# Cross-attention block on one core: the third batch's MLP by Strassen's scheme behind attention, with its rows kept in DRAM

## The chip, the cores and the metric

The kernel runs on one core of a Trainium2 chip. The core has TensorE (matrix products, in the profile PE, its weight loads PEld), VectorE (DVE), ScalarE (ACT), GpSimd (POOL) and SyncE (SP, here only a queue that issues transfers). Each engine works through its own instructions in order and waits for others by semaphores. The metric is the time of one execution in device microseconds; the median of several runs is compared.

## The reference

All values are fp32; batch 4, 512 rows, width 512, 16 heads of 32, inner width 2048.

```python
x = layer_norm(hidden_states, ln1_w, ln1_b)
q = (x @ q_w + q_b) ; k = (enc @ k_w + k_b) ; v = (enc @ v_w + v_b)   # split into 16 heads
attn = softmax(where(mask, q k^T / sqrt(32), min))
hidden = (attn v) @ cproj_w + cproj_b + hidden_states
y = layer_norm(hidden, ln2_w, ln2_b)
y = gelu(y @ fc_w + fc_b, approximate=True)
return hidden + y @ proj_w + proj_b
```

## The kernel before, in words

**Attention.** The work is cut into 16 groups w: batch b = w // 4 and four heads. A group has four units, one for each 128 query rows; unit u = 4 w + qt, 64 in all. A unit is `scores` (L207): four 32-row products into the single PSUM tile `sc`, VectorE's mask and row minimum of each head (L219, which frees `sc`), ScalarE's exp (L223), and then `turn` (L227), which transposes the four tiles. VectorE does this in 32x32 blocks (L251), and sixteen transfers on SP's queue (L274) put the blocks of two units (a pair) into the one tile `pT`; three pairs are transposed on TensorE instead and four use other tiles. `attend` (L297) multiplies a pair by v, four units after its first unit, and then VectorE multiplies by the inverse row sums (L322), the last reader of `pT`. Only then may the next pair's transfers start.

**The filler.** Between a unit's parts TensorE gets other work, in chains of four products of 512 columns: `prep_k`, `prep_q`, `prep_v` (three chains a group, three groups ahead), `cproj` of the batch that has just been attended (four chains and a VectorE sum into the row tiles `hid`), the second norm with its transposes (`ln2`, `ln2_turn`), and the MLP of the batch before: 16 `fc` chains (L377 on; gelu on ScalarE) and 16 `proj` chains (L390 on; a VectorE sum into `hid`, the last of which is stored). The lists `first[w]` are run from a group's first unit on, `later[w]` is added at the group's third unit. `run` takes items while their nominal costs (3.4 a chain, 0.5 a turn) fit into a quarter of the group's total, half of it before `turn` and half behind. The order that results is the order of every engine's queue: nothing is moved afterwards.

**Loads.** Weights are loaded by Pool's queue (`load_w`, `load_fc`, `load_p`, `load_hid`), each into a slot that its former reader must have left; Pool waits for that in its own order. `wk`, `wq` and `wv` have two slots each and are loaded together, one group ahead. `hid` has six slots, filled with the rows of x, to which Pool adds a bias (L339); a second bias is added on Pool after the norm (`proj_bias`, L362). The slots that are filled anew wait for the output store.

**The last MLP.** Batch 3's MLP has no attention beside it and is done by Strassen's scheme (Winograd's form): seven products of half-size blocks instead of eight. `fc_pair` (L466) does two of fc's 16 blocks; for it Pool forms four sums of the weight blocks (`a_sums`), VectorE four sums of y (`b_sums`, L555) and the sums of the products. `project` (L505) does the whole proj as seven products of 16 matmuls for each of two row tiles; the sums of the weights (`p_sums`) are Pool's, those of gelu's output (`g_sums`) VectorE's. The weights are loaded by SP's queue, pair by pair.

The norm of rows (`ln_stat`, `ln_rs`, `ln_norm`, L102 to L120) is: two VectorE instructions for each of four row tiles, two on Pool for rs, and four norms on VectorE.

Of the kernel before, what the change touches and what calls it, by code (L numbers as in the profile page):

```python
# [50 lines left out]
AHEAD = 3  # L52
LAG = 4
# [13 lines left out]
def xattn_block(ctx: ExitStack, tc: tile.TileContext, x, encT, mask, q_w, k_w, v_w, c_w, fc_w, p_w, vecs, rows, out):  # L67
# [6 lines left out]
    const, keep, hids, tiles, small = pools(ctx, const=1, keep=1, hids=6, tiles=4, small=4)  # L74
    ps_acc = ctx.enter_context(tc.tile_pool(name="ps_acc", bufs=4, space=PSUM))
# [90 lines left out]
    def load_w(w, queue=nc.gpsimd, names=("wk", "wq", "wv")):  # L166

        g = w % NG
        for n, src in (("wk", k_w), ("wq", q_w), ("wv", v_w)):
            if n in names:  # L170
                S[n, w] = two.tile([P, ND, P], F32, tag=n, name=f"{n}_{w}")
                queue.dma_start(out=S[n, w], in_=src[:, g, :, :])
# [10 lines left out]
    def prep_q(w):  # L183
        b, g = divmod(w, NG)
        qT = kqp.tile([P, L], F32, tag="qT", name=f"qT_{w}")
        acc = acc_tile(f"accq_{w}")
        for d in range(ND):
            nc.tensor.matmul(acc, S["wq", w][:, d, :], xT[:, d, :], start=(d == 0), stop=(d == ND - 1))  # L188

        nc.scalar.activation(qT, acc, AF.Identity, bias=qb[:, g : g + 1], scale=-scale)  # L190
        S["qT", w] = qT

    def prep_v(w):
# [3 lines left out]
        for t in range(NT):  # L197
            for d in range(ND):
                nc.tensor.matmul(  # L199
                    acc[:, ts(t, P)], eT[:, d, ts(t, P)], S["wv", w][:, d, :],  # L200
                    start=(d == 0), stop=(d == ND - 1),
                )
        nc.scalar.copy(v, acc.rearrange("p (t f) -> p t f", t=NT))
# [129 lines left out]
    def load_hid(b, ts_):  # L333

        for t in ts_:
            S["hid", b, t] = hids.tile([P, D], F32, tag="hid", name=f"hid_{b}_{t}")
            nc.gpsimd.dma_start(out=S["hid", b, t], in_=x[b, ts(t, P), :])
# [3 lines left out]
    def cproj(b, t):  # L341
# [3 lines left out]
        h = S["hid", b, t]  # L345
        nc.vector.tensor_tensor(h, acc, h, ALU.add)
        ln_stat((2, b), t, h)

    def ln2(b):
        if b + 1 < B:  # L350
# [4 lines left out]
        for t in range(NT):  # L355
            h = S["hid", b, t]
            ln_norm((2, b), t, S["yn", b][t], h)
# [6 lines left out]
    def ln2_turn(b, d):  # L364
        if d == 0 and b + 1 < B:
# [7 lines left out]
    def load_p(b, f):  # L373
        S["pw", b, f] = tiles.tile([P, D], F32, tag="pw", name=f"pw_{b}_{f}")
# [31 lines left out]
    def last_mlp(b, before):  # L406
# [5 lines left out]
        NP = NF // 2  # L412
        HL = L // 2

        last, ring = pools(ctx, last=1, ring=2)
        ps_last = ctx.enter_context(tc.tile_pool(name="ps_last", bufs=4, space=PSUM))

        yT = S["yT", b] = keep.tile([P, ND, L], F32, tag="yT", name=f"yT_{b}")
        ys = last.tile([P, 4, 2, HL], F32, tag="ys", name="ys")

# [3 lines left out]
        pt4 = last.tile([P, NP, HL], F32, tag="pt4", name="pt4")  # L424
        pt12 = gt[:, : 2 * NP * HL].rearrange("p (i c n) -> p i c n", i=2, c=NP)

# [3 lines left out]
        def sub(engine, o, x0, x1):  # L430
            engine.tensor_tensor(o, x0, x1, ALU.subtract)

        def a_sums(engine, a11, a12, a21, a22, s1, s2, s3, s4):
            engine.tensor_tensor(s1, a21, a22, ALU.add)
            sub(engine, s3, a11, a21)
            sub(engine, s2, s1, a11)
            sub(engine, s4, a12, s2)

        def b_sums(engine, b11, b12, b21, b22, t1, t2, t3, t4):
            sub(engine, t1, b12, b11)  # L440
            sub(engine, t2, b22, t1)
            sub(engine, t3, b22, b12)
            sub(engine, t4, b21, t2)

        def load(c):

            S["fa", c] = fa = ring.tile([P, 2, ND, P], F32, tag="fa", name=f"fa_{c}")
            for i in range(2):
                nc.sync.dma_start(out=fa[:, i], in_=fc_w[:, 2 * c + i, :, :])
            for i in range(2):  # L450
                nc.sync.dma_start(out=pb[:, c, i, :], in_=p_w[ts(2 * c + i, P), :])
            S["fs", c] = fs = ring.tile([P, 4, 2, P], F32, tag="fs", name=f"fs_{c}")
            a_sums(nc.gpsimd, fa[:, 0, :2], fa[:, 0, 2:], fa[:, 1, :2], fa[:, 1, 2:], *(fs[:, i] for i in range(4)))

        def p_sums(c):
# [3 lines left out]
            b_sums(nc.gpsimd, b11, b12, b21, b22, pt12[:, 0, c], pt12[:, 1, c], b12, pt4[:, c])  # L459

        def g_sums(c):
            c = slice(c, c + 2)
            a11, a12, a21, a22 = (ga[:, c, k, j * HL : (j + 1) * HL] for j in range(2) for k in range(2))
            a_sums(nc.vector, a11, a12, a21, a22, gs[:, 0, c], gs[:, 1, c], a21, gs[:, 2, c])

        def fc_pair(c):  # L466
            fa, fs = S["fa", c], S["fs", c]
            A = {(i, k): fa[:, i, 2 * k : 2 * k + 2] for i in range(2) for k in range(2)}
            Y = {(k, j): yT[:, 2 * k : 2 * k + 2, j * HL : (j + 1) * HL] for k in range(2) for j in range(2)}
            s1, s2, s3, s4 = (fs[:, i] for i in range(4))  # L470
            t1, t2, t3, t4 = (ys[:, i] for i in range(4))
            q1, q62 = (acc_tile(f"{n}_{c}").rearrange("p (i l) -> p i l", i=2) for n in ("q1", "q62"))
            q75, q43 = (half_tile(f"{n}_{c}") for n in ("q75", "q43"))
            p1 = ring.tile([P, HL], F32, tag="p1", name=f"p1_{c}")
            uc, u34, h = (ring.tile([P, 2, HL], F32, tag=n, name=f"{n}_{c}") for n in ("uc", "u34", "h"))
# [11 lines left out]

            product(q1[:, 0], A[0, 0], Y[0, 0])
            nc.scalar.copy(p1, q1[:, 0])
            product(q62[:, 0], s2, t2)  # L490
            product(q62[:, 1], A[0, 1], Y[1, 0])
            nc.vector.tensor_tensor(uc, q62, p1[:, None, :].broadcast_to([P, 2, HL]), ALU.add)
# [3 lines left out]
            nc.vector.tensor_tensor(u34, q75, uc[:, :1].broadcast_to([P, 2, HL]), ALU.add)  # L496
            nc.vector.tensor_tensor(uc[:, 0], q75[:, 1], u34[:, 0], ALU.add)
            gelu(1, 1, uc[:, 0])
            product(q43[:, 0], A[1, 1], t4)
            product(q43[:, 1], s4, Y[1, 1])  # L500
            nc.vector.tensor_tensor(h, q43, u34, ALU.add)
# [3 lines left out]
        def project():  # L505
            g11, g12, g21, g22 = (ga[:, :, k, j * HL : (j + 1) * HL] for j in range(2) for k in range(2))
            b11, b12, b21, b22 = (pb[:, :, k, j * HL : (j + 1) * HL] for k in range(2) for j in range(2))
            t1, t2, t3, t4 = pt12[:, 0], pt12[:, 1], b12, pt4
            s1, s2, s3, s4 = gs[:, 0], gs[:, 1], g21, gs[:, 2]
            q1, q6, q2 = (acc_tile(f"{n}p").rearrange("p (t n) -> p t n", t=2) for n in ("q1", "q6", "q2"))  # L510
            q7, q5, q4, q3 = (half_tile(f"{n}p") for n in ("q7", "q5", "q4", "q3"))
            p1 = last.tile([P, 2, HL], F32, tag="pp1", name="pp1")
            u2 = last.tile([P, 2, HL], F32, tag="pu2", name="pu2")
            u3 = last.tile([P, 2, HL], F32, tag="pu3", name="pu3")

            def product(o, a, w, t):
                for c in range(NP):
                    nc.tensor.matmul(o[:, t], a[:, c, ts(t, P)], w[:, c], start=(c == 0), stop=(c == NP - 1))
# [4 lines left out]
            def join(engine, i, j, src, t):  # L523
                engine.tensor_tensor(hid(i, j, t), src[:, t], hid(i, j, t), ALU.add)

            def store(i, j, t):
                nc.sync.dma_start(out=out[b, ts(2 * i + t, P), j * HL : (j + 1) * HL], in_=hid(i, j, t))

            for t in range(2):
                product(q1, g11, b11, t)  # L530
            nc.scalar.copy(p1, q1)
            for t in range(2):
                product(q6, s2, t2, t)
            nc.vector.tensor_tensor(u2, q6, p1, ALU.add)
            for t in range(2):
                product(q7, s3, t3, t)
            nc.vector.tensor_tensor(u3, q7, u2, ALU.add)
            for i, j, src in ((0, 0, p1), (0, 1, u2), (1, 0, u3), (1, 1, u3)):
                for t in range(2):
                    join(nc.gpsimd, i, j, src, t)  # L540
            for t in range(2):
                product(q5, s1, t1, t)
                join(nc.vector, 0, 1, q5, t)
                join(nc.vector, 1, 1, q5, t)
                store(1, 1, t)
            for q, x0, x1, i, j in ((q2, g12, b21, 0, 0), (q4, g22, t4, 1, 0), (q3, s4, b22, 0, 1)):
                for t in range(2):
                    product(q, x0, x1, t)
                    join(nc.vector, i, j, q, t)
                    store(i, j, t)  # L550

        load(0)
        load(1)
        run(before)
        b_sums(  # L555
            nc.vector, *(yT[:, 2 * k : 2 * k + 2, j * HL : (j + 1) * HL] for k in range(2) for j in range(2)),
            *(ys[:, i] for i in range(4)),
        )
        for c in range(NP):
            fc_pair(c)  # L560
            if c + 2 < NP:
                load(c + 2)
            if c % 2:
                p_sums(c - 1)
            elif c:
                g_sums(c - 2)
        g_sums(NP - 2)
        project()

# [7 lines left out]
    def A(w):  # L577
        if w >= NW:
            return []
        return do(lambda: load_w(w + 1) if w + 1 < NW else None) + [  # L580
# [48 lines left out]
    load_w(1)  # L629
# [144 lines left out]
```

## Time and profile before

| what | us |
|---|---|
| median of 3 runs | 856.24 (854.95 to 858.71) |
| the profiled execution, whole | 862.75 |
| its span, first to last instruction | 860.6 |
| attention, first to last scores | 24.3 to 686.5 |
| last MLP, first Strassen product to the end | 750.1 to 860.6 |

| engine | busy us | share |
|---|---|---|
| PE | 834.5 | 97% |
| DVE | 505.3 | 59% |
| ACT | 344.2 | 40% |
| POOL | 205.3 | 24% |

The durations that matter below, each the mean of its row among the groups of instructions: a VectorE sum of 128x512 0.69 us and of 128x256 0.42; a row minimum 0.69, of which the four of a unit follow each other every 0.61; a VectorE transpose 0.69 (2.5 for a unit's four); row statistics 0.69 and 0.18; a norm 0.54 in place and 1.00 with Pool at work beside it; a Pool sum 1.27 to 1.5; a transfer from pT's set 0.59 to issue. From issue to landing, in the median: pT 2.6, an output store 2.1, rows of x 4.1, weights of q 4.2.

How to read it: the timeline has one line for instructions of one kind that follow each other: start, length from the first start to the last end, engine and line, output and inputs, the number, and in brackets the idle time of the engine just before and what ended it. A dense fp32 product shows as two records. The profile was taken in one execution; its durations are used for differences, and these are added to the median.

### The profile page before, as it was taken

The page shows a single profiled execution, that of the slowest core. Times are in us where ns is not written, and L with a number is a line of the kernel's source. Part 1 is how long each engine was busy: PE and PEld are TensorE (multiplying, and loading weights), DVE is VectorE, ACT ScalarE, POOL GpSimd, SP SyncE. Part 2 cuts the span into 40 slices and gives each one's busy share as a digit, 9 for nine tenths or more (in the row PEclk, how much of TensorE's full clock was granted, in tenths as well). Part 3 has the DMA queues.
Part 4 walks back from the last instruction along what each step waited for, and adds up shares of the span by engine and source line. Part 5 has one row for each costly group of instructions (what it writes and reads, how often), then busy time and mean ns, then how long its engine had stood idle before and what let it go on. Part 6 is the DMA issues. An engine that isn't in the chain of part 4 may idle for free.

```text
span 860.6 us, 11545 instructions
## 1 busy us (share of the span) xinstructions
PE 834.5 (97%) x3914; PEld 443.1 (51%) x3914; DVE 505.3 (59%) x1127; ACT 344.2 (40%) x724; POOL 205.3 (24%) x293
## 2 busy tenths in 40 slices
PE   9999999989999999999999999999999999999997
PEld 6546555544454544545454444435444444487876
DVE  3596759974556356686456245696556741657610
ACT  2656555435635244324644334433645420023200
POOL 2211011541102003143201011123101102559710
PEclk9999999999999999999999999999999999999999
DMA  7357485675729465477755726566758683335000
GB/s 270 110 142 182 121 226 132 189 203 155 175 64 284 95 163 163 113 215 196 188 135 137 197 70 163 143 165 163 201 120 217 163 195 124 121 120 168 6 16 33
DMA packets 46457, 130.16 MB, mean 151 GB/s; under 512 B 11520, under 2 KB 12544, under 8 KB 46272
## 3 DMA queue, kind: packets, MB, share of 16 engines
q1 hardware_dynamic: 31248, 79.79, 36.7%
q0 software_dynamic: 14624, 48.51, 19.2%
q10 hardware_dynamic: 528, 1.14, 0.5%
q8 instruction: 31, 0.51, 0.3%
q14 instruction: 26, 0.21, 0.1%
HBM read 60.58 MB, written 4.19 MB: 75 GB/s over the span
## 4 chain that ended last, share of the span: by engine, by line
PE 78%; DMA 8%; DVE 7%; POOL 2%; SPq 2%; issue 2%; ACT 0%; DVEq 0%; POOLq 0%; ACTq 0%
PE accp L394 19%; PE accf L384 16%; PE av L317 6%; DMA pT<-tb 6%; PE sc L214 6%; PE accv L199 6%; PE accq L188 5%; PE acck L179 5%; PE accc L344 3%; PE q L479 3%; DVE s L219 3%; DVE tb L251 2%; SPq L274 2%; PE tp L127 2%; PE tpp L237 1%
## 5 line engine op out<-in xcount | busy, mean ns | idle before, releaser
L223 ACT ACTIVATE s<-s,mn 128x512 f32<-128x512 f32 x256 | 181.6, 710 | 152.9 <-DVE mn L219 152.6
L219 DVE CUSTOM_DVE_ANT_0 s<-sc,mb 128x512 f32<-128x512 f32 x256 | 161.0, 685 | 120.3 <-PE sc L214 120.0
L394 PE MATMUL accp<-pw,gt 128*128 128x512 f32 x384 | 171.3, 597 | 0.0
L384 PE MATMUL accf<-yT,fw 128*128 128x512 f32 x384 | 169.9, 596 | 0.0
L251 DVE STREAM_TRANSPOSE tb<-s 128x512 f32<-128x512 f32 x232 | 149.0, 686 | 2.7 <-ACT s L223 2.3
L384 PEld LDWEIGHTS accf<-yT,fw 128*128 128x128 f32 x384 | 71.7, 190 | 92.4 <-issue 89.3
L394 PEld LDWEIGHTS accp<-pw,gt 128*128 128x128 f32 x384 | 71.2, 190 | 92.3 <-issue 88.7
L398 DVE TENSOR_TENSOR hid<-accp,hid 128x512 f32<-128x512 f32 x48 | 32.8, 685 | 105.9 <-PE accp L394 105.9
L375 POOL DMA_DIRECT2D pw<-p_w_dram x48 | 25.8, 537 | 237.5 <-PE accp L394 237.5
L385 ACT ACTIVATE gt<-accf,vec 128x512 f32<-128x512 f32 x48 | 33.0, 687 | 107.6 <-PE accf L384 99.9
L214 PE MATMUL sc<-kT,qT 32*128 32x512 f32 x512 | 73.0, 640 | 2.4 <-DVE mn L219 1.6
L317 PE MATMUL av<-pT,v 128*32 128x256 f32 x896 | 57.3, 398 | 9.2 <-DMA pT<-tb 4.7
L199 PEld LDWEIGHTS accv<-wv,xe 128*128 128x128 f32 x512 | 58.8, 192 | 7.1 <-issue 3.4
L199 PE MATMUL accv<-wv,xe 128*128 128x128 f32 x512 | 60.7, 277 | 0.0
L179 PE MATMUL acck<-xe,wk 128*128 128x512 f32 x128 | 59.2, 603 | 0.3 <-DMA xe<-encT_dram 0.3
L188 PE MATMUL accq<-xe,wq 128*128 128x512 f32 x128 | 58.5, 599 | 0.0
L344 PE MATMUL accc<-wc,oT 128*128 128x512 f32 x128 | 56.8, 596 | 0.0
L371 POOL DMA_DIRECT2D fw<-fc_w_dram x48 | 25.9, 540 | 118.6 <-PE accf L384 110.3
L317 PEld LDWEIGHTS av<-pT,v 128*32 128x32 f32 x896 | 28.6, 113 | 45.3 <-issue 20.8
L223 ACT ACTIVATION_READ_ACCUMULATOR s<-s,mn 128x1 f32 x256 | 47.8, 187 | 0.0
L223 ACT ACT_TABLE_LOAD x21 | 26.9, 1283 | 37.0 <-DVE mn L219 37.0
L214 PEld LDWEIGHTS sc<-kT,qT 32*128 32x128 f32 x512 | 20.0, 182 | 41.4 <-issue 28.6
(118 smaller groups left out, 806.2 us busy)
## 6 DMA issues: line engine op xcount, KB each, us to landing
pT<-tb SPq DMA_DIRECT2D x400, 136.0 KB, 2.6
fw<-fc_w_dram POOLq DMA_DIRECT2D x48, 256.0 KB, 4.1
pw<-p_w_dram POOLq DMA_DIRECT2D x48, 256.0 KB, 3.4
gt<-tb SPq DMA_DIRECT2D x32, 136.0 KB, 3.4
hid<-x_dram POOLq DMA_DIRECT2D x16, 256.0 KB, 4.1
fa<-fc_w_dram SPq DMA_DIRECT2D x16, 256.0 KB, 3.0
pb<-p_w_dram SPq DMA_DIRECT2D x16, 256.0 KB, 3.8
wk<-k_w_dram POOLq DMA_DIRECT2D x15, 256.0 KB, 4.1
```

Source lines behind the costliest of these rows:

```text
L179: nc.tensor.matmul(acc, S["wk", w][:, d, :], eT[:, d, :], start=(d == 0), stop=(d == ND - 1))
L188: nc.tensor.matmul(acc, S["wq", w][:, d, :], xT[:, d, :], start=(d == 0), stop=(d == ND - 1))
L199: nc.tensor.matmul(acc[:, ts(t, P)], eT[:, d, ts(t, P)], S["wv", w][:, d, :], start=(d == 0), stop=(d == ND - 1),)
L214: nc.tensor.matmul(sc[:, h, :], qT[r, ts(qt, P)], kT[r, :], start=True, stop=True)
L219: nc.vector.tensor_tensor_reduce(out=s, in0=sc[:, h, :], in1=S["mb", w // NG], scale=1.0, scalar=FMAX, op0=ALU.add, op1=ALU.min, accum_out=mn,
L223: nc.scalar.activation(s, s, AF.Exp, bias=mn, scale=-1.0, accum_out=sums[:, qt, h : h + 1])
L251: nc.vector.transpose(tv[:, q, h], S["ps", w, qt][h])
L317: nc.tensor.matmul(av[ts(h, HD), : 2 * P].rearrange(shape, **kw), v[:, t, ts(h, HD)], p[t][h], start=(t == 0), stop=(t == NT - 1),)
L344: nc.tensor.matmul(acc, S["oT", b][:, g, ts(t, P)], wc[:, g, :], start=(g == 0), stop=(g == NG - 1))
L384: nc.tensor.matmul(acc, S["fw", b, f][:, d, :], S["yT", b][:, d, :], start=(d == 0), stop=(d == ND - 1))
L385: nc.scalar.activation(gT[q % 2][:, k, :], acc, AF.Gelu_apprx_tanh, bias=vec[:, FCB + f : FCB + f + 1], scale=1.0)
L394: nc.tensor.matmul(acc, gT[q % 2][:, k, ts(t, P)], S["pw", b, q * FQ + k], start=(k == 0), stop=(k == FQ - 1))
```

## The change

1. **Which MLPs are dense.** Only batches 0 and 1 (`NORMAL = 2`) run their MLP as filler in attention. Their 64 chains are one list, dealt out by `some(n)`: groups with no cproj get eight chains (three of q, k, v and five of the MLP, or eight of the MLP). The MLPs of batches 2 and 3 follow attention, one after the other, both by Strassen's scheme (`last_mlps`).
2. **Rows in DRAM.** From batch 1 on, `cproj` adds onto a tile `ct` (two slots) loaded with x's rows by Pool, and stores the sum by SP's queue into a DRAM tile; the load of row tile t + 2 is issued in `cproj` of t. The rows are loaded into `hid` (or, for batch 3, into `hl`) when their norm is near, and the statistics are taken there.
3. **The norms behind attention.** Batch 2's stands in the last cproj; batch 3's, its transposes and its y sums are emitted in `middle`, between the products q5 and q4 of batch 2's proj.
4. **Sums.** All sums of weight blocks are VectorE's. The fc weights and their sums lie in `gt`, two pairs deep, and are loaded and summed for each batch; the proj weights are loaded at once (16 transfers on SP) and summed once, in `sums`.
5. **proj's products** are ordered anew (q1, q2, q3, q6, q7, q5, q4), each for both row tiles before its joins.
6. **wq and wv** have one slot each and are loaded when the former product has been emitted.

```diff
+NORMAL = 2
...
+                S[n, w] = (two if n == "wk" else one).tile([P, ND, P], F32, tag=n, name=f"{n}_{w}")
...
+        load_w(w + 1, names=("wq",))
...
     def cproj(b, t):
...
-        h = S["hid", b, t]
+        h = S["hid", b, t] if b == 0 else S["ct", b, t]
         nc.vector.tensor_tensor(h, acc, h, ALU.add)
-        ln_stat((2, b), t, h)
+        if b == 0:
+            ln_stat((2, b), t, h)
+            return
+        nc.sync.dma_start(out=S["xa", b][ts(t, P), :], in_=h)
+        if t + 2 < NT:
+            load_ct(b, t + 2)
+
+    def load_ct(b, t):
+        if t == 0:
+            S["xa", b] = dram.tile([L, D], F32, tag=f"xa{b}", name=f"xa{b}")
+        S["ct", b, t] = two.tile([P, D], F32, tag="ct", name=f"ct_{b}_{t}")
+        nc.gpsimd.dma_start(out=S["ct", b, t], in_=x[b, ts(t, P), :])
...
+    def sum_wa(c):
+        a = wa[c % 2]
+        a_sums(a[:, 0, :2], a[:, 0, 2:], a[:, 1, :2], a[:, 1, 2:], *(ws[c % 2][:, i] for i in range(4)))
...
+            gelu(1, 1, uc[:, 0])
+            sums()
+            product(q43[:, 1], s4, y22)
+            product(q43[:, 0], a22, t4)
...
+            product(q5, s1, t1)
+            join(nc.vector, 0, 1, q5)
+            join(nc.vector, 1, 1, q5)
+            store(0, 1)
+            store(1, 1)
+            middle()
+            q4 = half_tile(f"q4p_{b}"), acc_half(f"q4p_{b}")
...
+            def middle(b=b):
+                if b + 1 < B:
+                    stat2(b + 1, range(NT))
+                    ln2(b + 1)
+                    run(turns2(b + 1))
+                    y_sums(b + 1)
+                    sum_wa(0)
...
+    first[10] = [load, k, q] + some(5) + [v]
...
+    first[12] = ct(2) + stat(1, 0, 1) + [load, k] + stat(1, 2, 3) + some(1) + norm(1)
+    later[12] = c[:2] + t2[:2] + c[2:3] + t2[2:] + bias(1) + c[3:] + some(2)
+    first[13] = [q] + some(3) + [v] + some(3)
+    first[14] = hid_(2, 0, 1) + some(8)
+    first[15] = some(8)
...
+    stat2(2, (0, 1))
+    run(some(1))
+    load_wa(0)
+    load_wa(1)
+    stat2(2, (2, 3))
+    run(c[:1])
+    ln2(2)
+    run(c[1:])
+    sum_wa(0)
     att.close()
-    last_mlp(b, p3[2:] + turns2(b) + do(lambda: proj_bias(b)))
+    last_mlps()
```

In the same way `first[8]` holds three chains of q, k, v, one MLP chain and batch 3's first norm, and `later[8]` the four cproj chains of batch 1; groups 5 to 7, 9 and 11 have five MLP chains each.

## The prediction

> **What bounds the kernel now.** I read the page's busy shares and its chain that ended last first:
>
> ```profile
> PE 834.5 (97%) x3914; PEld 443.1 (51%) x3914; DVE 505.3 (59%) x1127; ACT 344.2 (40%) x724; POOL 205.3 (24%) x293
> ...
> PE 78%; DMA 8%; DVE 7%; POOL 2%; SPq 2%; issue 2%; ACT 0%; DVEq 0%; POOLq 0%; ACTq 0%
> ```
>
> TensorE is the bound, the others are hidden behind it. So a change pays by what it takes off TensorE, and costs by every wait it puts into TensorE's order. The price of work comes from the timeline of the end (columns: start, length, engine, line):
>
> ```profile
> 701.57 10.57 PE L394 MATMUL accp<-pw,gt 128*128 128x512 f32 x24
> 711.98 7.03 PE L384 MATMUL accf<-yT,fw 128*128 128x512 f32 x16
> 718.84 3.60 PE L394 MATMUL accp<-pw,gt 128*128 128x512 f32 x8
> ...
> 762.23 1.03 PE L479 MATMUL q<-yT,fa 128*128 128x256 f32 x4
> 768.27 1.03 PE L479 MATMUL q<-yT,fa 128*128 128x256 f32 x4
> 805.12 7.07 PE L518 MATMUL q1p<-pb,ga 128*128 128x256 f32 x32
> 812.03 7.07 PE L518 MATMUL q6p<-gt,gs 128*128 128x256 f32 x32
> 838.07 3.72 PE L518 MATMUL q2p<-pb,ga 128*128 128x256 f32 x16 [0.52 <-DVE hid L524]
> ```
>
> From start to start: two dense chains (16 records) take 718.84-711.98 = 6.86, one 3.43 us. A Strassen pair of fc takes 768.27-762.23 = 6.04, one Strassen product of proj 6.91.
>
> **1. The work.** Batch 2's MLP is 32 dense chains, 32 x 3.43 = 109.8 us. By Strassen it is 8 x 6.04 + 7 x 6.91 = 96.7. That is **-13.1**, all on TensorE.
>
> **2. Waits that go.** The old proj joins after each half product; TensorE waited 0.92 us once and 0.52 three times: **-2.5**. The fc waits for Pool's weight sums were 1.55 and 0.23 us. On VectorE a pair's work is 3 x 0.69 + 0.42 + 4 x 0.42 for weight sums = 4.2 us, 6.9 where four g sums (0.69) join it, against 6.04: it runs late by some 0.5 us three times a batch, 3 us in the two batches. I take **+1.2** net (ends -1.8 and +5; the upper one if the 4 MB of proj weights hold up the third pair's weights).
>
> **3. The middle: batch 3's second norm.** It is emitted between q5 and q4 of batch 2's proj, on each engine's queue. Transposes stand ahead of q4 on TensorE, and VectorE reaches the statistics only after q5's joins. The same chain in the profile, at the end of attention:
>
> ```profile
> 742.49 0.69 DVE L106 BATCH_NORM_STATS2 st<-hid 128x6 f32<-128x512 f32 x1
> 743.49 0.19 POOL L112 TENSOR_SCALAR ve<-mv 128x4 f32<-128x4 f32 x1 [7.39 <-DVE mv L107]
> 743.77 1.04 POOL L114 TENSOR_TENSOR rs<-ve,nhalf 128x4 f32<-128x4 f32 x1
> 744.84 3.55 DVE L118 TENSOR_SCALAR xn<-hid,mv,rs 128x512 f32<-128x512 f32 x4 [1.44 <-POOL rs L114]
> 748.37 1.93 PE L127 MATMUL tp<-ident,xn 128*128 128x128 f32 x16
> 753.56 1.72 PE L479 MATMUL q<-ys,fs 128*128 128x256 f32 x4 [2.40 <-DVE ys L431]
> ```
>
> There two dense proj chains covered it. Here nothing does: four joins x 0.42 = 1.7, four statistics x (0.69 + 0.18) = 3.5, Pool 1.44, four norms x 0.54 (the row without Pool beside it) = 2.2: 8.9 us of idle TensorE. The evictions, y sums and weight sums that follow (some 8 us on VectorE) lie beside q4's 6.9. After such a gap the clock is low:
>
> ```profile
> 749.00:753.60 4.60, 2.21 (x17) 1.74 (x15) 4.46 (x6) 1.93 (x3) 4.52 (x5) 1.00 0.31 116
> 753.60:757.00 3.40, 3.40 (x9) 2.72 (x10) 3.16 (x2) 0.00 (x0) 3.40 (x3) 0.54 0.00 0
> ```
>
> After a wait of 2.40 us the granted clock (third number from the end) is 0.54 for 3.4 us, so half of that, 1.7 us, is lost. **+10.6** (ends 8 and 13). The Trainium skill, "TensorE: Matmul & The Clock Gate", Part 1, says that the clock falls after an idle window of about 3.4 us; this row shows it after 2.40. By the page the entry's short wait of before would have cost no clock and the longer one of step 4 would: the total would be 1.7 us more.
>
> **4. Rows of cproj through DRAM.** The mechanism stands in the profile already, where rows are loaded into slots that an output store must leave:
>
> ```profile
> 545.66 10.04 SPq L274 DMA_DIRECT2D pT<-tb  x16
> 555.81 1.61 SPq L400 DMA_DIRECT2D out_dram<-hid  x2
> 558.77 0.55 POOL L337 DMA_DIRECT2D hid<-x_dram  x1 [16.69 <-DMA out_dram<-hid]
> ```
>
> SP's queue is in order: a store emitted after a pair's 16 pT transfers goes out behind them, and these wait for the single pT tile, freed by the product with the row sums (L322) after the previous attend. Pool's queue stands still until the store has landed. In the change, cproj's first row (c0) is stored on SP behind a pair's transfers; the load for the third row (c2) waits on Pool for that slot; VectorE's c2 sum waits for the load, and all of VectorE's queue for it. After L322: 10.1 (transfers) + 0.35 + 2.1 (store, median to landing) + 4.1 (load, ditto) = **17 us**, while the c2 product is done some 11 us after.
>
> *Group 12 (units 48 to 51).* Its list for the first two units holds only two chains, both spent in unit 48 (10.0 us, as 628.40 to 638.40), so unit 49 has scores alone, 1.3. Unit 50's scores need unit 49's row minima. VectorE has ahead of them, from unit 48's start: minima to 3.7, L322 0.4, four statistics 3.5, transposes 2.5, a proj sum 0.7, norms 2.7, minima 2.5: 16.0, against TensorE's 11.3: 4.8 idle. Then L322 comes at 22.3, behind transposes and minima, the c2 sum at 22.3 + 17 = 39.4; behind it transposes 2.5, an eviction 0.8, a sum 0.7, unit 51's minima 2.5: unit 52's scores at 46 to 48.6 (with 1.7 for the clock). Without waits the group takes 2 x 10.0 + 2 x 8.13 + four turns 1.9 = 38. So 8 to 10.6; before, the same stretch lost 2.0 (0.35 at 557.75, 1.67 at 577.62). **+8.4**, near the upper value, since VectorE's list holds no slack (ends 2 and 11).
>
> *Group 8.* Here the first two units are full, and VectorE is held some 5 us by c2; unit 37's scores and unit 38's attend come late, the latter because its pT transfers start later: 0.7 + 3.4 at most before the clock. I take **+3** (0 and 7).
>
> *The entry to the MLPs.* From the last attend's end: the last proj chain and C0 end at 6.9, C0's sum at 7.8, its store lands at 10.3. Only then Pool, which waits there to load row 2, does the norm's rs (1.44 and the 0.54 of issuing): 12.3. Norms to 14.5, C1's sum 15.2, store landed 17.6, row 3's load landed 21.7, C3's sum 22.4, weight sums with Pool's bias adds beside them 2.5, two evictions 1.6, two y sums 1.4: 28. TensorE ends C3 at 17.2 and has 3.5 us of turns and products to do: 7.3 idle, where it was 2.40. **+4.9** (ends 0 and 7); the low clock follows both. The Trainium skill, "DMA: Bandwidth & Descriptors", Anatomy of one DMA, gives 2.0 us + bytes / 436e3, an estimate of 2.6 us for these 256 KB loads; the rows' median is 4.1. With 2.6 the entry and group 12 would each be 1.5 us cheaper, the total 3.
>
> **5. One tile for wq and wv.** The second wq is issued when the first q product ends (23.8) instead of before it, and lands 4.4 later (median) at 28.2; the second q product started at 25.37. Up to 2.8; VectorE is nearly full in the next units and gives some back. **+2** (0 and 3).
>
> **6. Pairs of units with eight chains a group** last 18.1 us (629.47 to 647.60 between attends). pT's loop (minima and L322 3.0, issue 10.0 to 14.8, landing 2.6) needs 15.6 and up; the pair at 459.97 would not have fitted. The waits at 480.55 (1.98 and the clock) go, some elsewhere come: **-1.3** (-4 and +6).
>
> Counted at nothing: the statistics moved out of cproj, the MLP weights' later loads on Pool, and yT and pw in other pools lie beside TensorE's dense chains (VectorE is busy 59%, Pool 24%); without that cover the eight statistics would be 7 us. The end is as before: one sum and one store behind the last product.
>
> Sum: -13.1 - 2.5 + 1.2 + 10.6 + 8.4 + 3 + 4.9 + 2 - 1.3 = **+13.2 us**. The profiled execution took 862.75 (span 860.6 and 2.15 around); the median of the runs is 856.24, so I add the difference to that: 869.4.
>
> **Rivals.** *A, faster:* VectorE's holds fit into TensorE's slack, so that step 4 costs only unit 49's 2.5 us (minima after scores), the second q wait is made up and the middle costs 8.9: -13.1 - 2.5 + 8.9 + 2.5 - 1.3 = -5.5, 850.7. For it: cproj waited 2.24 us for Pool at 376.00, and TensorE lost nothing. Against: the 16.69 above. It decides where the c2 load lands before VectorE gets to c2's sum, at about 11 us instead of 17. *B, no change:* half of step 4 (8.1) and step 5 at 1: 856.24 - 13.1 - 2.5 + 1.2 + 10.6 + 8.1 + 1 - 1.3 = 860.2; a little milder and it is level. *C, much slower:* pT's loop becomes the bound of the tight groups. With some 20 such pairs and 0.5 us more at each, +10: 879.4. For it: the issue of 14.8. Against: the pairs at 18.1 us had no wait. *D, it does not do what it says:* Strassen's products run slower than 6.04 and 6.91; no reason in the rows, 1 in 100.
>
> **Chances.** Forecast 0.51 (all of it slower), A 0.2, B 0.18, C 0.1, D 0.01 (beyond C). Within 0.5% (4.3 us), which is what a measurement here can tell from none, falls half of B and a little of A: same 0.14; faster 0.2; slower 0.66. The range takes in A and C: 850 to 881.
>
> **What would show it.** Right: an idle TensorE of about 9 us ahead of batch 3's transposes; Pool's rs at the entry released by the store of the rows; VectorE's third cproj sum released by a DMA, and scores of units 50 and 52 waiting for minima; TensorE's busy time without its gaps some 13 us shorter, with 256 dense records gone and 448 new ones. Wrong: those sums released by TensorE, or less than 4 us of idle in the middle.

## The result and the profile after

| | us |
|---|---|
| before, median of 4 runs | 856.30 (854.95 to 858.71) |
| after, median of 4 runs | 880.37 (879.13 to 882.17) |
| after / before | 1.028 (95% interval 1.025 to 1.0309) |
| the profiled execution after, whole and span | 880.17 and 878.4 |

Slower, as forecast, and 11.0 us longer than forecast (869.4), inside the range. The page of the changed kernel (engines, granted clock in 40 slices, the chain's shares, then two groups with their idle time and its releaser):

```profile
PE 826.1 (94%) x4106; PEld 481.6 (55%) x4106; DVE 552.9 (63%) x1255; ACT 346.1 (39%) x745; POOL 149.1 (17%) x229
...
PEclk9999999999999999999997999999998999899999
...
PE 68%; DMA 10%; DVE 9%; SPq 7%; issue 5%; POOL 1%; ACT 0%; DVEq 0%; POOLq 0%; ACTq 0%
...
L406 PE MATMUL accf<-yT,fw 128*128 128x512 f32 x256 | 115.4, 600 | 5.2 <-DVE yT L133 5.2
L324 PE MATMUL av<-pT,v 128*32 128x256 f32 x896 | 58.0, 402 | 14.2 <-DMA pT<-tb 9.9
```

TensorE is busy 8.4 us less than before, and the chain that ended last has gone over to transfers, VectorE and SP's queue (26% together, 17% before). Three slices show a lower clock; before had none. Attends wait 14.2 us, 9.9 of them for pT transfers.

To see where the time went I cut the span at the first scores of each group and subtracted from each stretch its matmul records, each at the interval in which it usually follows. The remainder is waiting and low clock. After less before, us, by the prediction's steps; the last column uses a second profile of the unchanged kernel (run e1 below):

| stretch | predicted | against the profile shown | against its repeat |
|---|---|---|---|
| TensorE's work (1) | -13.1 | -13.1 | -13.1 |
| behind the last scores: 2, the middle (3), the entry (4) | +14.2 | +9.9 | +9.8 |
| group 12 (4) | +8.4 | +12.6 | +12.6 |
| groups 8 to 10 (4) | +3 | +5.9 | +5.9 |
| start and groups 0, 1 (5) | +2 | +0.7 | +1.2 |
| the other groups (6) | -1.3 | +1.8 | +6.0 |
| sum | +13.2 | +17.8 | +22.4 |

**The middle** reads as forecast. VectorE's joins, statistics and norms stand one behind the other, Pool's rs between them, and TensorE's transposes wait 6.76 us for the first norm; with Pool's bias adds beside them two of the norms take 1.49 and 1.48 instead of 0.54, so two more waits of 0.93 follow:

```profile
758.17 1.42 DVE L483 TENSOR_TENSOR hid<-q5p,hid 128x256 f32<-128x256 f32 x4 [6.29 <-PE q5p L547]
...
763.16 1.03 POOL L117 TENSOR_TENSOR rs<-ve,nhalf 128x4 f32<-128x4 f32 x1
764.23 3.81 DVE L121 TENSOR_SCALAR xn<-hl,mv,rs 128x512 f32<-128x512 f32 x4 [1.44 <-POOL rs L117]
764.83 0.93 PE L130 MATMUL tp<-ident,xn 128*128 128x128 f32 x2 [6.76 <-DVE xn L121]
```

**The entry** too: Pool issues the load of `ct` only when the store has landed (7.22), rs and the norms come behind it, and the sum that needs the next load waits 5.83. TensorE's third fc product waits 6.05 (7.3 forecast):

```profile
651.03 0.56 POOL L366 DMA_DIRECT2D ct<-x_dram  x1 [7.22 <-DMA xa<-ct]
...
653.02 1.91 DVE L121 TENSOR_SCALAR xn<-hid,mv,rs 128x512 f32<-128x512 f32 x4 [5.62 <-POOL rs L117]
...
661.96 0.69 DVE L354 TENSOR_TENSOR ct<-accc,ct 128x512 f32<-128x512 f32 x1 [5.83 <-DMA ct<-x_dram]
...
665.90 2.93 PE L511 MATMUL q<-yT,gt 128*128 128x256 f32 x6 [6.05 <-DVE yT L133]
```

**Group 12**, in the timeline from unit 50's scores on:

```profile
464.62 2.09 PE L221 MATMUL sc<-kT,qT 32*128 32x512 f32 x8 [4.65 <-DVE mn L226]
...
471.04 3.64 PE L324 MATMUL av<-pT,v 128*32 128x256 f32 x32 [4.33 <-DMA out_dram<-hid]
...
474.73 0.42 DVE L329 TENSOR_TENSOR oT<-av,pT 128x256 f32<-128x256 f32 x1 [4.45 <-PE av L324]
475.19 10.04 SPq L281 DMA_DIRECT2D pT<-tb  x16
...
485.33 10.89 SPq L358 DMA_DIRECT2D xa<-ct  x4
...
491.50 0.69 DVE L354 TENSOR_TENSOR ct<-accc,ct 128x512 f32<-128x512 f32 x1 [7.93 <-DMA ct<-x_dram]
```

The scores wait 4.65 us for row minima (4.8 forecast). From the product with the row sums to the third cproj sum it is 491.50 - 474.73 = 16.8 us (17 forecast). But between the two stands a wait that the forecast did not have: the attend of pair 23 waits 4.33 us more. SP had issued the 16 transfers for this pair from 452.94 to 465.07, but they landed late: the last of them at 470.58. The release is put down to a store issued behind them on the same queue, which landed only at 471.21, when the attend had begun. From issue to landing these 16 transfers took 6.6 us in the median, with six loads of Pool's queue (`wv`, two of `ct`, three of `fw`) beside them, and those of the next pair, without loads beside them, 2.4 (columns: transfer, queue, number, KB, median us to landing):

```profile
pT<-tb SPq DMA_DIRECT2D x16, 136.0 KB, 6.6
```

```profile
pT<-tb SPq DMA_DIRECT2D x16, 136.0 KB, 2.4
```

After both waits the attend itself takes 3.64 instead of 1.93.

**Group 5** holds the surprise. In the changed kernel, and then in the kernel before:

```profile
193.72 0.54 POOL L177 DMA_DIRECT2D wv<-v_w_dram  x1 [8.99 <-PE accv L205]
...
194.27 4.91 POOL L384 TENSOR_TENSOR hid<-hid,row 128x512 f32<-128x512 f32 x4
...
194.67 4.68 DVE L265 COPY rr<-rsum 128x256 f32<-128x256 f32 x1
...
200.58 1.13 PE L406 MATMUL accf<-yT,fw 128*128 128x512 f32 x2 [4.14 <-DVE yT L133]
```

```profile
179.05 0.54 POOL L172 DMA_DIRECT2D wv<-v_w_dram  x1
181.02 3.80 DVE L118 TENSOR_SCALAR xn<-hid,mv,rs 128x512 f32<-128x512 f32 x4
181.64 5.54 POOL L362 TENSOR_TENSOR hid<-hid,row 128x512 f32<-128x512 f32 x4 [2.06 <-DVE xn L118]
```

Before, all weights of a group were issued together, and Pool's four bias adds (`proj_bias`) ran beside the norms. Now wv's single slot makes Pool wait 8.99 us for the v product, and the adds stand behind that load on Pool's queue. They start 17.0 us behind the group's first scores instead of 8.3, and a VectorE copy of 0.29 us meets them: it ends 0.17 us after the last of the four and takes 4.68. The eviction behind it is late, and the dense product waits 4.14.

The low clock behind each of these waits (columns: window, length, busy time and records of PE, PEld, DVE, ACT, POOL, then the granted clock):

```profile
201.80:205.20 3.40, 3.40 (x24) 1.03 (x28) 1.54 (x5) 1.39 (x2) 1.06 (x2) 0.50 0.56 187
465.00:475.20 10.20, 5.87 (x41) 2.11 (x38) 5.64 (x16) 3.87 (x12) 0.00 (x0) 0.52 0.53 137
662.60:669.40 6.80, 3.50 (x8) 2.86 (x9) 6.42 (x11) 0.37 (x1) 1.10 (x1) 0.50 0.59 184
761.60:771.80 10.20, 5.11 (x19) 4.07 (x20) 6.37 (x10) 1.55 (x2) 6.76 (x6) 0.50 0.00 0
```

### The profile page after: what moved, and what is told of

It reads as the page before. It is cut to its first block, busy times and chain, and to the rows that moved or that the text cites. A ratio compares the mean times of both kernels' runs of the same rounds, so it can differ in the third digit from the quotient of the medians.

```text
span 878.4 us, 12059 instructions
## 1 busy us (share of the span) xinstructions
PE 826.1 (94%) x4106; PEld 481.6 (55%) x4106; DVE 552.9 (63%) x1255; ACT 346.1 (39%) x745; POOL 149.1 (17%) x229
## 4 chain that ended last, share of the span: by engine, by line
PE 68%; DMA 10%; DVE 9%; SPq 7%; issue 5%; POOL 1%; ACT 0%; DVEq 0%; POOLq 0%; ACTq 0%
PE q L511 10%; PE accp L416 9%; PE accf L406 7%; SPq L281 6%; PE av L324 6%; DMA pT<-tb 6%; PE sc L221 5%; PE accv L205 5%; PE acck L184 4%; PE accq L193 4%; PE accc L352 4%; DVE s L226 3%; DVE tb L258 2%; PE q4p L547 2%; PE q5p L547 2%
## 5 line engine op out<-in xcount | busy, mean ns | idle before, releaser
L258 DVE STREAM_TRANSPOSE tb<-s 128x512 f32<-128x512 f32 x232 | 147.2, 684 | 2.5 <-ACT s L230 2.3
L406 PE MATMUL accf<-yT,fw 128*128 128x512 f32 x256 | 115.4, 600 | 5.2 <-DVE yT L133 5.2
L416 PE MATMUL accp<-pw,gt 128*128 128x512 f32 x256 | 114.9, 599 | 0.7 <-DMA pw<-p_w_dram 0.7
L406 PEld LDWEIGHTS accf<-yT,fw 128*128 128x128 f32 x256 | 46.9, 190 | 68.8 <-issue 54.9
L416 PEld LDWEIGHTS accp<-pw,gt 128*128 128x128 f32 x256 | 47.2, 190 | 64.5 <-issue 60.4
L324 PE MATMUL av<-pT,v 128*32 128x256 f32 x896 | 58.0, 402 | 14.2 <-DMA pT<-tb 9.9
L511 PE MATMUL q<-ys,gt 128*128 128x256 f32 x256 | 60.9, 381 | 0.0
L511 PE MATMUL q<-yT,gt 128*128 128x256 f32 x192 | 48.5, 389 | 6.8 <-DVE yT L133 6.0
L420 DVE TENSOR_TENSOR hid<-accp,hid 128x512 f32<-128x512 f32 x32 | 21.9, 686 | 51.2 <-PE accp L416 51.2
L511 PEld LDWEIGHTS q<-ys,gt 128*128 128x128 f32 x256 | 49.0, 192 | 6.9
L135 ACT ACTIVATE yT<-tp,vec 128x512 f32<-128x512 f32 x8 | 6.2, 774 | 99.0 <-PE tp L130 98.9
```

The source lines that it names most:

```text
L258: nc.vector.transpose(tv[:, q, h], S["ps", w, qt][h])
L324: nc.tensor.matmul(av[ts(h, HD), : 2 * P].rearrange(shape, **kw), v[:, t, ts(h, HD)], p[t][h], start=(t == 0), stop=(t == NT - 1),)
L406: nc.tensor.matmul(acc, S["fw", b, f][:, d, :], S["yT", b][:, d, :], start=(d == 0), stop=(d == ND - 1))
L416: nc.tensor.matmul(acc, gT[q % 2][:, k, ts(t, P)], S["pw", b, q * FQ + k], start=(k == 0), stop=(k == FQ - 1))
L511: nc.tensor.matmul(o, a[:, k], y[:, k], start=(k == 0), stop=(k == 1))
```

## The experiments

My theory: the Strassen work pays its 13.1 us, and the loss is several separate waits (middle, entry, group 12, start, and then group 5), each of which can be undone by order alone. Rivals: the sums on VectorE are what costs; or pT's loop sets the pace of all tight groups, so that no order helps. Ratios below are to the kernel before on the same chip, where its median was 854.7 to 858.6 us; the changed kernel's ratio is 1.028. Gains by stretch come from the profiled executions.

**e1, the kernel before again.**

> The kernel before, unchanged, for a second profile of it: its first one took 862.75 us against a median of 856.3. If the 6.5 us between are waits of that one execution, this profile has a span near 854 and lacks some of the first one's waits for the pT transfers (at 177 and 480 us, about 4.2 and 3.7 us with the low clock behind them). If profiling itself costs it, the span is near 860 again.

858.05 us, span 855.9. It loses 2.6 us less in group 5 and 2.9 less in group 11 (the attend at 480.55 of the prediction) than the first profile, and 1.3 more in group 7. So these waits are not a fixed part of the kernel.

**e2, the norm of batch 3 before q5's products.**

```diff
             add(nc.vector, u3p, q7, u2p)
+            norm()
...
+            def norm_next(b=b):
                 if b + 1 < B:
                     stat2(b + 1, range(NT))
                     ln2(b + 1)
+            def middle(b=b):
+                if b + 1 < B:
                     run(turns2(b + 1))
```

> Batch 3's statistics and norm are put on the queues ahead of q5's joins, so that VectorE does them beside the product q5; only the transposes stay between q5 and q4. If the middle's wait is VectorE's chain behind q5 (my theory), TensorE's idle time ahead of those transposes falls from about 10 us with the slow transposes to under 2, and the low clock behind it goes: 880.4 becomes 869 to 871. If VectorE is too full in that stage (the rival: all sums on VectorE are what costs), the norm only delays q5's joins or the y sums, and less than 4 us are won.

872.02 us, 1.018 (1.0132 to 1.0229), just above the 869 to 871 of the theory; behind the last scores 9.4 us less. Statistics, rs and norms now lie beside q5:

```profile
752.57 7.07 PE L547 MATMUL q5p<-pt,gs 128*128 128x256 f32 x32
...
757.03 1.03 POOL L117 TENSOR_TENSOR rs<-ve,nhalf 128x4 f32<-128x4 f32 x1
...
759.48 0.27 PE L130 MATMUL tp<-ident,xn 128*128 128x128 f32 x1
```

The transposes follow the product at once. The middle's cost was the uncovered chain.

**e3, a full group 12.** The cproj chains and turns fill its first units, so that unit 49 is not empty.

```diff
-    first[12] = ct(2) + stat(1, 0, 1) + [load, k] + stat(1, 2, 3) + some(1) + norm(1)
-    later[12] = c[:2] + t2[:2] + c[2:3] + t2[2:] + bias(1) + c[3:] + some(2)
+    first[12] = ct(2) + stat(1, 0, 1) + [load, k] + stat(1, 2, 3) + some(1) + norm(1) + t2 + some(2)
+    later[12] = c[:3] + bias(1) + c[3:]
```

> Group 12's first two units get the four turns and the two MLP chains that stood at its end, so that unit 49 is not empty. My theory: unit 50's scores no longer wait for unit 49's row minima (4.7 us and part of the low clock), the hold by the third cproj sum remains or grows by a little: 880.4 becomes 873 to 877. Rival (the loop of the single pT tile sets the pace in this group): attend at unit 50 waits as long as before for its transfers, under 2 us are won.

880.73 us, 1.0288 (1.0235 to 1.0342): nothing won. Group 12 lost 6.8 us less, group 13 5.9 more:

```profile
483.15 10.04 SPq L281 DMA_DIRECT2D pT<-tb  x16
...
493.30 7.08 SPq L358 DMA_DIRECT2D xa<-ct  x3
496.30 0.55 POOL L366 DMA_DIRECT2D ct<-x_dram  x1 [19.23 <-DMA xa<-ct]
...
499.35 0.69 DVE L354 TENSOR_TENSOR ct<-accc,ct 128x512 f32<-128x512 f32 x1 [6.56 <-DMA ct<-x_dram]
...
506.26 0.42 DVE L329 TENSOR_TENSOR oT<-av,pT 128x256 f32<-128x256 f32 x1
...
521.31 3.64 PE L324 MATMUL av<-pT,v 128*32 128x256 f32 x32 [4.85 <-DMA xa<-ct]
```

The store still goes out behind the 16 transfers, the load behind the store; VectorE is held, frees pT 8 us after the attend at 498.25, and the next attend waits. The wait had only moved.

**e4, the rows stored by Pool's queue.**

```diff
-        nc.sync.dma_start(out=S["xa", b][ts(t, P), :], in_=h)
+        nc.gpsimd.dma_start(out=S["xa", b][ts(t, P), :], in_=h)
```

> The rows of cproj are stored by Pool's queue instead of SP's, so that they do not stand behind the sixteen pT transfers. My theory: the load of the third row lands about 10 us earlier, VectorE's third cproj sum is held under 3 us instead of some 6 to 8, and group 12 gets 5 to 8 us shorter: 872 to 876. Rival (VectorE's amount of work there, not the queue): the third sum may come earlier, but unit 51 and 52 start as late as before; under 2 us.

883.28 us, 1.0315 (1.0259 to 1.037): a miss. The third sum waits 3.29 instead of 7.93, but the wait in front of it stays, and the stretch behind the last scores loses 6 us more. Most of that is the entry: rs comes no later there, but Pool's four bias adds now stand behind the stores on its queue and meet VectorE's sums of weight blocks. One of these three sums takes 5.47 us instead of 0.42, and TensorE's fc product waits 10.23 instead of 6.05:

```profile
474.77 3.64 PE L324 MATMUL av<-pT,v 128*32 128x256 f32 x32 [4.93 <-DMA out_dram<-hid]
...
491.05 0.69 DVE L354 TENSOR_TENSOR ct<-accc,ct 128x512 f32<-128x512 f32 x1 [3.29 <-DMA ct<-x_dram]
...
664.45 6.27 DVE L439 TENSOR_TENSOR gt<-gt 128x256 f32<-128x256 f32 x3
...
665.06 4.91 POOL L384 TENSOR_TENSOR hid<-hid,row 128x512 f32<-128x512 f32 x4
...
671.50 2.93 PE L511 MATMUL q<-yT,gt 128*128 128x256 f32 x6 [10.23 <-DVE yT L133]
```

**e5, both together** (e3's lists; Pool stores the rows of batches 1 and 2, SP those of batch 3).

> In this kernel group 12 gives the batch's blocks to the units as group 11 ended them (its list is that of the run with the fuller group 12) and batch 1's and 2's rows of the output projection go to DRAM on Pool's queue; batch 3's stay on SP's. If the store behind 16 pT transfers and the order of group 12 are two locks on one loop (each alone moved the wait), both edits together take most of groups 12 and 13: 8 to 13 us less than the changed kernel, 867 to 872. If the pT loop itself sets the pace there (a pair's transfers take 10 us of its 18 whatever is stored between), less than 3 us are won: 877 to 881.

875.52 us, 1.0231 (1.0185 to 1.0277). Group 12 lost 8.9 us less, group 13 3.8 more: half of what was expected, between theory and rival. What took the rest is read under e7.

**e6, entry, middle and start.** e2's edit, and:

```diff
-    run(c[:1])
     ln2(2)
-    run(c[1:])
+    run(c)
...
-    load_w(1, names=("wk",))
+    load_w(1, names=("wk", "wq"))
```

(the second group's wq into the tile of `oT`, not yet in use).

> Three places outside the tight groups, all at once: batch 3's statistics and normalisation go before the projection's last products (9.4 us less when done alone), batch 2's reciprocal root goes ahead of the load that Pool's queue held it behind (theory: the entry's 6 us of idle and its clock fall to the 2 of the kernel before, 4 us less), and the second group's q weights are loaded at the start into a buffer that is not yet in use (theory: 1 to 2 us). Sum: 864 to 867. If the entry's wait is passed on to the next thing on VectorE, as happened in group 12, only the middle is won: 869 to 872.

865.88 us, 1.0112 (1.0077 to 1.0147). Behind the last scores 14.2 us less, of which e2 alone gave 9.4, so the entry gives 4.8; group 0 gives 1.9. The fc product that waited 6.05 now waits 1.97, since rs is ahead of the load on Pool:

```profile
642.91 1.04 POOL L117 TENSOR_TENSOR rs<-ve,nhalf 128x4 f32<-128x4 f32 x1
...
658.09 1.56 PE L515 MATMUL q<-yT,gt 128*128 128x256 f32 x6 [1.97 <-DVE yT L133]
```

**e7, e5 and e6 together.**

> All five edits of the other kernels together. If their waits are separate, the gains add: 880.4 less 9.4 (middle), 4 (entry), 1 to 2 (start) and 8 to 13 (groups 12 and 13) gives 852 to 858, level with the kernel before or just below it, which is what 13 us less TensorE work and about 8 to 12 us of waits left in the tight pairs would give. If the pT loop sets the pace of the groups, 862 to 868.

861.20 us, 1.0055 (1.0028 to 1.0082), between the two expectations: the gains add, but e5's missing half is missing here too. At the end of its group 12:

```profile
485.02 4.94 POOL L388 TENSOR_TENSOR hid<-hid,row 128x512 f32<-128x512 f32 x4
...
485.46 4.66 DVE L269 COPY rr<-rsum 128x256 f32<-128x256 f32 x1
...
493.54 0.42 DVE L333 TENSOR_TENSOR oT<-av,pT 128x256 f32<-128x256 f32 x1
```

The same meeting as in group 5 of the changed kernel, this time made by my new order: four adds of Pool, a copy of 4.66, and pT freed 6.9 us after its attend began. The next attend waits 7.09 us for its transfers.

**e8, the weight sums of fc on Pool** (the rival that sums on VectorE cost the time).

```diff
-        a_sums(a[:, 0, :2], a[:, 0, 2:], a[:, 1, :2], a[:, 1, 2:], *(ws[c % 2][:, i] for i in range(4)))
+        a_sums(a[:, 0, :2], a[:, 0, 2:], a[:, 1, :2], a[:, 1, 2:], *(ws[c % 2][:, i] for i in range(4)), engine=nc.gpsimd)
```

> The sums over the fc weights are made by Pool in place of VectorE (the same sums, 64 of 512 columns); nothing else is changed. If sums on VectorE are what costs the time (the rival), 3 to 8 us are won: 872 to 877. If, as the trace of the changed kernel reads, TensorE waits little for them (0.6 to 0.8 us where it waits in that stage), the time is within 2 us of the changed kernel or longer, since Pool is slower at a sum and slows VectorE beside it: 879 to 885.

882.91 us, 1.0315 (1.0277 to 1.0353); behind the last scores 1.1 us more. The rival is out for these sums: Pool's are slower (0.77 us each in place of 0.42), and the fc products wait for them:

```profile
684.14 2.86 PE L511 MATMUL q<-ys,gt 128*128 128x256 f32 x12 [0.82 <-POOL gt L439]
```

**e10, in the changed kernel only batch 0's bias adds taken apart**, one row tile behind each dense product.

```diff
-        for t in range(NT):
-            h = S["hid", b, t]
-            nc.gpsimd.tensor_tensor(h, h, row[:, 1, :], ALU.add)
+        h = S["hid", b, t]
+        nc.gpsimd.tensor_tensor(h, h, row[:, 1, :], ALU.add)
...
-    first[5] = norm(0) + [load, q, k] + t2[:3] + [v] + t2[3:] + bias(0) + some(5)
+    first[5] = norm(0) + [load, q, k] + t2[:3] + [v] + t2[3:] + mix(some(5), bias(0))
```

> The changed kernel with one edit: batch 0's projection bias in group 5 one row block at a time. Theory: in the changed kernel the four adds stand on Pool's queue behind the v weights' load, which waits for the v product, and so meet the copy that the kernel before never showed them with. Without that: 4.1 us of TensorE idle and 1 to 2 us of low clock in group 5 go, 874 to 876. If group 5's loss is the pT loop's and the copy is only beside it: 878 to 881.

876.46 us, 1.0245 (1.0197 to 1.0293), just above the 874 to 876 of the theory. This interval overlaps that of the changed kernel, so the gain is read from the stage: group 5 lost 5.5 us less and group 6 0.9 more. (Group 0, ahead of the edit, lost 1.9 more in this execution, by a low clock.) The copy meets no add and is at its 0.29 again, and the dense products run through:

```profile
194.94 3.62 PE L405 MATMUL accf<-yT,fw 128*128 128x512 f32 x8
...
195.91 0.29 DVE L265 COPY rr<-rsum 128x256 f32<-128x256 f32 x1
...
196.57 1.28 POOL L383 TENSOR_TENSOR hid<-hid,row 128x512 f32<-128x512 f32 x1
```

**e9, e7 with the bias adds of batches 0 and 1 taken apart.**

> The kernel with all five edits, and the projection's bias added by Pool one row block at a time, each behind a dense product, in place of four in a row (batch 0 in group 5, batch 1 in group 13). Theory: the four adds in a row held a VectorE copy for 4.66 to 4.69 us where they met it (0.29 otherwise), once in group 5 and once in group 12; TensorE waited 4.1 us behind the first and 7.7 behind the second, with 1 to 3 us of low clock after each. Without them: 861.2 less 5 to 6 and less 8 to 9, 846 to 849, below the kernel before (856.1). If the copy was only late beside something that is late anyway (the pT transfers, the next load), at most half comes: 854 to 858.

849.49 us, 0.993 (0.9905 to 0.9955): faster than the kernel before by 6.5 us, or 0.7%. Against e7, group 5 loses 6.9 us less and group 13 8.5 less, group 6 3.3 more; the median, 11.7 less, is just above what was expected. The page:

```profile
PE 819.8 (97%) x4106; PEld 477.6 (56%) x4106; DVE 550.9 (65%) x1255; ACT 346.3 (41%) x745; POOL 155.9 (18%) x237
...
PEclk9999999999999999999999999999999999999999
```

TensorE's share and the clock are those of the kernel before. Its span is 8.4 us shorter than that of e1: 13.1 less work, 4.7 more waiting.

**e11, e9 with the projection's weights loaded one or two at a time** behind the dense products of the next quarter, for what is left in group 10.

> The 849.5 us kernel with one more edit: the projection's second and third quarter of weights (4 loads of 256 KB each, issued within 2.6 us when the last product of a quarter frees their buffers) are issued one or two at a time behind the dense products that follow. Theory: what is left in groups 6 and 10 (waits of 2.5 and 2.8 us for pT transfers that were issued on time, and the low clock after the first) is DMA time shared with these loads and the fc loads; spreading them wins up to 3 us in group 10 and leaves group 6: 846 to 848.5. If a pair's transfers land late for another reason, or the product that needs the last weights now waits for them: 849 to 853.

854.66 us, 0.9969 (0.9942 to 0.9996): nothing won, a miss; the interval overlaps that of e9 (0.9905 to 0.9955). The attend that waited 2.82 us for pT in e9 no longer waits, but the next pair does, and so does one in group 15 (3.19). First e9, then e11:

```profile
368.93 1.93 PE L328 MATMUL av<-pT,v 128*32 128x256 f32 x32 [2.82 <-DMA pT<-tb]
```

```profile
386.10 1.93 PE L328 MATMUL av<-pT,v 128*32 128x256 f32 x32 [1.56 <-DMA pT<-tb]
```

That loads delay a pair's landing is in keeping with this; that spreading them pays is not.

## Why the prediction was right or wrong

**Right: direction, and the main mechanisms.** The work (step 1) is exact. Middle and entry were forecast at 10.6 and 4.9, and undoing them gave 9.4 and 4.8. Step 2's net was too dear: with these two taken off, the stretch behind the last scores is 4.3 us better than before (9.9 - 9.4 - 4.8), and 1.3 was forecast; the fc stage's price of VectorE's sums (+1.2) did not come (its lower end was -1.8). (There I set VectorE's lateness at 0.5 us a time, where my own 6.9 against 6.04 gives 0.9.) Rival A fell with the 16.8 us hold, B with the size of step 4's waits, D with the work.

**Too low by 11.0, for two reasons.** 6.3 is the step "I add the difference to that". The profiled execution was 6.5 us longer than the median, and I treated this as a constant. 5.5 of it were waits in groups 5 and 11 that the repeat lacks, and step 6 even counted one of them, at 480.55, as a gain of the change. The other 4.6 are terms:

- *Step 6 (pairs), wrong in sign: +1.8 or, by the repeat, +6.0 for -1.3.* The failed step is the list of what is "counted at nothing": it has the MLP weights' later loads on Pool, but not the later load of wv. I priced wq's single slot (step 5) by the product that waits for it, but not what stands behind the moved wv load on Pool's queue. That was the bias adds, and with them the copy: 5.5 us by e10. Another 3.2 us are lost in group 4 (one attend waits 2.87 us for transfers that took 13.87 to issue and, beside five loads of Pool's queue, 6.8 in the median to land). In all kernels with the change's order group 4 loses 1.7 to 5.0 more than before; its cause was not tried and is open.
- *Step 4, group 12: 12.6 for 8.4.* Both times that I worked out (4.8 and 17) came to within 0.2 us. Missing is the attend's own wait, 4.33 us and its clock, because I followed the hold on VectorE and left out that the pair's transfers were late as well. (The terms of that step also reach only 46 + 1.7 = 47.7, not 48.6, so they support 7.7 at most.) e3 to e9 show two locks here (the empty unit and the store behind the transfers), and taking both away together (e5, e7) brought a third (the bias adds). Taking one moved the wait; with none left (e9), groups 12 and 13 lose 9.7 us less to waiting and low clock than in the changed kernel.
- *Step 4, group 8: nothing there.* The hold on VectorE came (the row sums' product of pair 16 is 7.1 us after its attend), but the 5.9 were lost in groups 9 and 10, where pairs found their transfers late. With the rows on Pool (e5) group 9 is without a wait, so its 1.4 were the price of the hold. Group 10 keeps 3.3 of its 4.5 in e5: in the changed kernel its transfers are issued in 10.2 us without a stop, but the last four land some 9 us after their issue, beside five loads of Pool's queue. The sum has no term for that.
- *Step 5: 1.9 for 2*, given back in part later. The agreement is in part luck: in five later profiles with the same order there (e2, e3, e4, e8, e10) the low clock followed this wait, and group 0 lost 3.3 to 4.8.

**Rival C is not what happened**, though its figure (879.4) is the closest. In the changed kernel the attends of pairs 26, 27 and 28 start at 538.97, 557.11 and 575.24, 18.13 apart with nothing waited for, and the transfers for the second are issued by 552.05. So the loop fits into a full pair. It passed on delays from elsewhere (group 9 here, group 13 in e3 and e7). Where transfers landed late on their own account (groups 4, 10 and 12), loads of Pool's queue lay beside them; that the loads are the cause is read from these traces and not shown by an experiment, and e11's spreading of some of them settled nothing.

## What to carry to other kernels

A load that is given a later release moves everything behind it on its queue: list what else that engine does there, and what those instructions will now meet. When a wait has several locks, undoing one alone shows nothing; follow the wait to where it went before dropping the theory. And before a difference is added to a median, see by a second profile which waits belong to the one execution only.

## What the runs showed of the hardware

- A VectorE copy of 128x256 fp32 (0.29 us) that meets a row of Pool sums ends with the last of them: 4.68 and 4.66 us beside four adds of 4.91 and 4.94, 4.11 where it came later. The Trainium skill, "SBUF — State Buffer", Who interferes with whom, says that VectorE and GpSimd share a port pair and that, where both need it, the second is blocked for the whole of the first one's instruction. The blocking agrees; but one add of 1.28 would have held the copy no longer than that, and here it was all four. Taken apart (e10), the adds did not meet the copy.
- A VectorE sum of 128x256 with both inputs in SBUF is held in the same way: 5.47 us instead of 0.42 in e4, 1.42 in the changed kernel's entry, each time to 0.29 us after the last add. Norms and sums of 128x512 beside such a row became only about 1 us longer each (0.54 to 1.49, 0.69 to 1.75). What makes the difference was not tried.
- The low clock (0.50 to 0.52) lasted 3.4, 6.8 or 10.2 us, multiples of one step, behind the waits of 4.1 to 6.8 us shown above; it lasted longest, 10.2, where further waits followed the first, of 4.33 us in group 12 and of 0.93 twice in the middle. In e4 it lasted 13.7 behind the wait of 10.23. The length of a wait alone does not decide: in e9 the attend behind a wait of 2.53 us (group 6) met the low clock and took 3.60 us, the one behind 2.82 (group 10) did not and took 1.93.
